# Soft-disc layer of a four-layer kernel: from pairs of blocks to columns of four, sums of exponentials as products with ones, the quotient at the result copy, values through DRAM

## The chip, the cores and the metric
The kernel runs on one core of one Trainium2 chip. The metric is the device time of one execution in microseconds (us). All data are float32.

## What is computed
Four residual layers work one after another on 8 images of 32 x 32 tokens with 256 channels. Each is `x = x + layer(groupnorm(x))`. The change lies in the last one, a windowed attention with a soft disc as mask. Cut to what matters:

```python
def _L3_conv_ref(x, w_qkv, w_qn, w_kn, w_wp, b_wp, w_on, w_out):   # 8 heads of 32 channels, window 7 x 7
    qkv = silu(x @ w_qkv.T)
    q, k, v = split(qkv, 3, axis=-1)
    q = apply_rope(rms_norm(q, w_qn));  k = apply_rope(rms_norm(k, w_kn))
    wp = silu(x @ w_wp.T + b_wp)                      # two numbers per token and head
    width, sharp = sigmoid(wp_1) * max_dist + 0.5, sigmoid(wp_2) * 9.5 + 0.5
    k_win, v_win = unfold2d(k), unfold2d(v)           # zero padding of 3 on each side
    scores = einsum('blhd,blwhd->blhw', q, k_win) * D ** -0.5
    soft_mask = sigmoid((width - rel_dist) * sharp)
    attn = softmax(scores - (1.0 - soft_mask) * 10000.0, axis=-1)
    out = rms_norm(einsum('blhw,blwhd->blhd', attn, v_win), w_on)
    return silu((out + v) @ w_out.T)
```

## The kernel before
**Layers 0 to 2** (`layer0`, `layer1`, `layer2`) are not touched. Layer 2 is a windowed attention too, and it already works in steps of a column of four blocks (`NearStream`, L1655 to L1768): scores L1677, logits L1688, exponentials L1700, quotient on POOL L1705, transposes L1720 with their copies L1724, products with the values L1741, result copy L1748. Its values go through DRAM (stores L1959, fetches of windows L1763).

**Layer 3** is `layer3` (from L2075) with `DiscStream` (from L1771). Channels stand on the partitions and tokens on the free axis. An image's 1024 tokens are 16 blocks of 8 x 8, in 4 columns of 4. The work is cut into 16 chunks J: image b = J // 2 and half of the heads c = J % 2 (4 heads of 32 channels, so 128 partitions). A chunk has 8 groups; a group n is a pair of blocks one above the other, with 128 queries in all on the partitions, so there are 128 groups. Each block sees a window of 14 x 14 = 196 keys.

A group goes through these stages:
- `soft` (L2217, ACT): four tanh, one per head, that write the mask from the distances of a window; width and sharpness of a query are bias and scale.
- `masked` (L2224, POOL): adds the window's hard limits for all four heads at once.
- `scores` (L1802, PE): 8 products, 2 blocks by 4 heads, into four PSUM banks `s`.
- `logits` (L1815, DVE): per head, scores plus mask into the tile `e`, with the minimum as accumulated output `mx`.
- `exps` (L1825, ACT): per head the exponential in place, with the row's sum as accumulated output `su`. The profile shows the reading of that accumulator as an instruction of its own, ACTIVATION_READ_ACCUMULATOR.
- `divide` (L1832 DVE, L1833 POOL): reciprocal of the 4 sums, and e times it.
- `turn` (L1843 PE, L1848 DVE): 4 heads by 2 parts of transposes in two PSUM banks `pt`, each copied to `pts`. A part is 112 keys: 8 rows of 14. The tile e has a row of 14 zeros ahead of the 196 columns and another behind them, so two parts cover the window of either block.
- `values` (L1859 PE, L1867 DVE): 12 products of the turned weights with the values into one bank `o` (4 heads by the three value tiles that the pair's rows touch), and two copies of a block each to the result `oT`.

The values of a chunk are prepared so: `project` makes `vT`; `in_strips` (L2275, POOL, two copies) lays it out in four strips of 14 columns with padding; five units `vturn` (L1876 PE, L1881 DVE) transpose 20 tiles of 112 keys into `v`.

Other work of a chunk: six `project` units (L2141 PE, tanh `half_silu` L2126 on ACT, then DVE L2151 or L2153 from the PSUM bank, squares on POOL L2161); `roots` (sums of squares L2236 and L2243 on PE, and at once a table load, logarithm L2251 and exponential L2252 on ACT); `head_scale` (L2260 PE, L2265 DVE), twice with two banks each. Per image: `load`, group norm (`gn`), `normed` (L418), `discs` (L2174 and after), `tail_sq` (L2289), `tail_scale` (L2295, L2300, L2303), `output` (L2311, L2318, L2320) and `reload`.

**What sets the order.** The block is recorded with `tc.manual_schedule`: PE, ACT, DVE and POOL execute in the order in which the Python code calls them. All PSUM tiles of layer 3 come from one ring of eight banks: an allocation waits until the eighth one before it is released. The loop (L2431) takes group n through a staggered pipeline: scores and logits of n + 3, exponentials of n + 1, quotient of n, turn of n - 2, values of n - 3, mask of n + 5. Between them stand the other units: `Fillers` (L439) holds them with a due time in steps, and `units(at)` emits those that are due. A unit that has a second half (DVE and POOL work that waits for PE or ACT) returns it, and `finish` calls it at the next such point. Transfers are issued by SP in the order of recording, each behind its own waits.

Of the kernel before, what the change touches and what calls it, by code (L numbers as in the profile page):

```python
# [1770 lines left out]
class DiscStream(Stream):  # L1771

# [5 lines left out]
    def __init__(self, K, wk, cp, pp, pairs, n_img, ebufs):  # L1780
        super().__init__(K, wk, pp, pairs, n_img, ebufs)
        self.slots, self.s, self.su = 20, {}, {}
        shape = [P, 4, 2 * self.PART]
        self.tiles = [cp.tile(shape, F32, name=f"e{i}") for i in range(ebufs)]

# [6 lines left out]
    def prob(self, n):  # L1792
        return self.tile(n)[:, :, self.ROW : self.ROW + NWIN]

    def scores(self, n):
        b, c, t = self.groups[n]
        s = [self.ring(f"s{j}") for j in range(4)]
        q, k = self.q[b, c], self.k[b, c]
        for g in range(2):
            for j in range(4):  # L1800
                ch = slice(32 * j, 32 * j + 32)
                self.nc.tensor.matmul(  # L1802
                    grid(s[j][64 * g : 64 * g + 64, :NWIN], self.ROW),
                    q[ch, 64 * t.block(g) : 64 * t.block(g) + 64],
                    k[ch, t.krs[g] : t.krs[g] + self.ROW, t.kc : t.kc + self.ROW],
                    start=True, stop=True,
                )
        self.s[n] = s

    def logits(self, n):  # L1810

        s, e = self.s.pop(n), self.prob(n)
        self.mx[n] = self.wk.tile([P, 4], F32, name="mx", bufs=self.ebufs)
        for j in range(4):
            self.nc.vector.tensor_tensor_reduce(  # L1815
                e[:, j], in0=s[j][:, :NWIN], in1=e[:, j], scale=MASK_SCALE,
                scalar=3.0e38, op0=ALU.add, op1=ALU.min,
                accum_out=self.mx[n][:, j : j + 1],
            )

    def exps(self, n):
        mx, e = self.mx.pop(n), self.prob(n)
        su = self.su[n] = self.wk.tile([P, 4], F32, name="su", bufs=4)
        for j in range(4):
            self.nc.scalar.activation(  # L1825
                e[:, j], e[:, j], AF.Exp, scale=-1.0, bias=mx[:, j : j + 1],
                accum_out=su[:, j : j + 1],
            )

    def divide(self, n):  # L1830
        e, su = self.prob(n), self.su.pop(n)
        self.nc.vector.reciprocal(su, su)  # L1832
        self.nc.gpsimd.tensor_mul(e, e, su.unsqueeze(2).to_broadcast([P, 4, NWIN]))  # L1833

    def turn(self, n, i):

        if i == 0:
            self.pts[n] = self.wk.tile([P, 2, HALF], F32, name="pts", bufs=2)
        ps = self.ring("pt")
        for j in range(2):  # L1840
            for k in range(2):
                at = (2 * j + k) * P
                self.nc.tensor.transpose(  # L1843
                    ps[: self.PART, at : at + P],
                    self.tile(n)[:, 2 * i + j, k * self.PART : (k + 1) * self.PART],
                    self.K.ident,
                )
        self.nc.vector.tensor_copy(self.pts[n][: self.PART, i, :], ps[: self.PART, :])  # L1848

    def values(self, n):  # L1850
        b, c, t = self.groups[n]
        pts = self.pts.pop(n)
        v, at = self.v[b, c], 5 * t.col + t.rows[0]
        o = self.ring("o")

        for k, q0, o0, w in ((1, 64, 0, P), (0, 0, 64, 64), (2, 192, 0, 64)):
            for j in range(4):
                p0 = (j % 2) * 2 * P + q0
                self.nc.tensor.matmul(  # L1859
                    o[32 * j : 32 * j + 32, o0 : o0 + w],  # L1860
                    v[: self.PART, at + k, 32 * j : 32 * j + 32],
                    pts[: self.PART, j // 2, p0 : p0 + w],
                    start=k == 1, stop=k != 1, skip_group_check=True,
                )
        for g in range(2):
            d = self.o[b, c][:, t.token(g) : t.token(g) + 1]
            self.nc.vector.tensor_copy(  # L1867
                bass.AP(d.tensor, d.offset, [d.ap[0], [SIDE, 8], [1, 8]]),
                o[:, 64 - 64 * g : 128 - 64 * g].rearrange("p (i j) -> p i j", j=8),
            )  # L1870

    def value_unit(self, strips, dst, u):
        ps = self.ring("vt")
        for i in range(4):
            col, r = divmod(4 * u + i, 5)
            self.nc.tensor.transpose(  # L1876
                ps[: self.PART, i * P : i * P + P],
                strips[:, col, 8 * r : 8 * r + 8].rearrange("p i j -> p (i j)"),
                self.K.ident,
            )  # L1880
        return lambda: self.nc.vector.tensor_copy(  # L1881
            dst[: self.PART, 4 * u : 4 * u + 4, :],
            ps[: self.PART, :].rearrange("p (s c) -> p s c", c=P),
        )
# [190 lines left out]
def layer3(tc, K, src, dst, n_img, a, first):  # L2075
    nc = tc.nc
    pairs = disc_pairs()
    with tc.tile_pool(name="l3c", bufs=1, reuse_waits="tile") as cp, tc.tile_pool(
        name="l3w", bufs=1, reuse_waits="tile"
    ) as wk, tc.tile_pool(name="l3p", bufs=1, space=PSUM, reuse_waits="tile") as pp:  # L2080
        x, xq, vT, disc, xr, fac, sqs = {}, {}, {}, {}, {}, {}, {}
# [6 lines left out]
        kpad = [cp.tile([P, PADW, PADW], F32, name=f"kp{i}") for i in range(3)]  # L2088
        strips = cp.tile([P, 4, PADW + 2, 14], F32, name="strips")
        for t in (kpad[0], strips):  # L2090
            nc.gpsimd.memset(t, 0.0)
        st = DiscStream(K, wk, cp, pp, pairs, n_img, 9)
        for i in range(3):
            st.clear(i)
        K.ring = st.ring
# [33 lines left out]
        def project(J, s, h):  # L2129
            b, c = divmod(J, 2)  # L2130
            if h == 0:
                if s == 0:
                    st.q[b, c] = wk.tile([P, L], F32, name="qT", bufs=3)
                elif s == 1:
                    st.k[b, c] = kpad[J % 3]
                else:
                    vT[b, c] = wk.tile([P, L], F32, name="vT", bufs=5)
# [74 lines left out]
        def soft(n):  # L2212
            b, c, t = st.groups[n]
            i, e = pairs.index(t), st.prob(n)
# [7 lines left out]
        def masked(n):  # L2222
            e = st.prob(n)
            nc.gpsimd.tensor_add(e, e, win[:, 1].unsqueeze(1).to_broadcast([P, 4, NWIN]))  # L2224

        def roots(J, b):
# [19 lines left out]
            n = P if heads else 64  # L2248
# [6 lines left out]
        def head_scale(J, s):  # L2255

            ps = [st.ring("fac_ps") for _ in range(2)]
            for h in range(2):
                g = slice(32 * (2 * s + h), 32 * (2 * s + h) + 32)
                nc.tensor.matmul(ps[h], spread[g, s], fac[J][g], start=True, stop=True)  # L2260

            def rest():
                for h in range(2):
                    d = dest(J, s, h)
                    nc.vector.tensor_mul(d, d, part(ps[h]))  # L2265

            return rest

        def in_strips(J):
            b, c = divmod(J, 2)  # L2270
            v = grid(vT[b, c], SIDE)
            for out, first, step, n in ((3, 0, 21, 11), (560, 5, 8, 14)):
                i, o = v[:, 0:1, first : first + 1], strips[:, 0:1, 4:5, 0:1]
                ostep = 3 * 560 - 3 if n == 11 else 560
                nc.gpsimd.tensor_copy(  # L2275
                    bass.AP(o.tensor, o.offset + out, [o.ap[0], [ostep, 2], [14, SIDE], [1, n]]),
                    bass.AP(i.tensor, i.offset, [i.ap[0], [step, 2], [SIDE, SIDE], [1, n]]),
                )

        def vturn(J, u):  # L2280
            b, c = divmod(J, 2)
            if u == 0:
                st.v[b, c] = wk.tile([P, st.slots, P], F32, name="v", bufs=2)
            return st.value_unit(strips, st.v[b, c], u)


# [4 lines left out]
        def tail_scale(J, b, h):  # L2291

            g, hs = slice(32 * h, 32 * h + 32), slice(h * HALF, (h + 1) * HALF)
            ps = st.ring("fac_ps")
            nc.tensor.matmul(ps, ones[g], fac[J][g], start=True, stop=True)  # L2295

            def rest():
                for c in range(2):
                    d = st.o[b, c][:, hs]
                    nc.vector.scalar_tensor_tensor(  # L2300
                        d, d, on[:, c : c + 1], ps, ALU.mult, ALU.mult
                    )
                    nc.gpsimd.tensor_add(d, d, vT[b, c][:, hs])  # L2303
# [29 lines left out]
        def plan_chunk(J):  # L2333

            n, (b, c) = 8 * J, divmod(J, 2)
            if J == 0:
                return
            for i in range(4):
                s, h = 1 - i // 2, i % 2
                fill.add(n - 12 + i / 2, lambda s=s, h=h: project(J, s, h))  # L2340
            for s in range(2):
                fill.add(n - 5 - s, lambda s=s: head_scale(J, s))
            fill.add(n - 8.5, lambda: project(J, 2, 0))
            fill.add(n - 8, lambda: project(J, 2, 1))
            fill.add(n - 6, lambda: in_strips(J))

        def plan_image(b):
            n = 16 * b
            if b:
                fill.add(n - 27.5, lambda: load(b))  # L2350
# [169 lines left out]
```

## Time and profile before

| what | us |
|---|---|
| median of 3 runs | 3138.45 (3135.41 to 3157.48) |
| the profiled execution: its time | 3142.47 |
| its span, first to last instruction | 3140.7 |
| layer 2's last scores | 2356.8 |
| layer 3's first and last scores (start) | 2403.6 and 3090.8 |
| layer 3's first and last products with the values (start) | 2434.4 and 3111.6 |

The mean granted TensorE clock is 0.979 of full speed. Instructions of layer 3 by engine, duration from the groups of 2374 to 3141 us, and start to start where the next instruction of the engine follows without idleness:

| instruction | count | mean duration, us | start to start, us |
|---|---|---|---|
| ACT tanh of the mask, L2217 | 512 | 0.541 | 0.442 |
| ACT exponential L1825 to its accumulator read | 512 | 0.447 | 0.349 |
| ACT accumulator read to the next | 512 | 0.190 | 0.093 |
| ACT table load, L2250 | 18 | 1.283 | |
| POOL mask L2224 | 128 | 1.601 | 1.57 |
| POOL quotient L1833 | 128 | 1.498 | 1.456 |
| DVE logits L1815 (each with its accumulator read) | 512 | 0.354 | 0.28 |
| DVE copy of pts, L1848 | 256 | 0.678 | 0.597 |
| DVE copy of a value unit, L1881 | 80 | 0.678 | 0.598 |
| DVE result copy of a block, L1867 | 256 | 0.212 | 0.132 |
| DVE reciprocal of 128 x 4, L1832 | 128 | 0.166 | 0.085 |
| DVE copy of 128 x 2, L205 | 32 (whole kernel) | 0.145 | 0.063 (least 0.045) |
| DVE 128 x 256 from PSUM, L2153 | 128 | 0.415 | 0.332 |

[...] On PE the profile writes a float32 product as two records and a transpose as one, and neighbouring records of one line as one group with the number of records. "Idle before" with an arrow names what ended the idle time. A wait for a PSUM bank appears as a wait for the instruction that released it.

### The profile page before, as it was taken

The page shows a single profiled execution, that of the slowest core. Times are in us where ns is not written, and L with a number is a line of the kernel's source. Part 1 is how long each engine was busy: PE and PEld are TensorE (multiplying, and loading weights), DVE is VectorE, ACT ScalarE, POOL GpSimd, SP SyncE. Part 2 cuts the span into 40 slices and gives each one's busy share as a digit, 9 for nine tenths or more (in the row PEclk, how much of TensorE's full clock was granted, in tenths as well). Part 3 has the DMA queues.
Part 4 walks back from the last instruction along what each step waited for, and adds up shares of the span by engine and source line. Part 5 has one row for each costly group of instructions (what it writes and reads, how often), then busy time and mean ns, then how long its engine had stood idle before and what let it go on. Part 6 is the DMA issues. An engine that isn't in the chain of part 4 may idle for free. (4 is left out here: it accounts for less than half of the span.)

```text
span 3140.7 us, 76133 instructions
## 1 busy us (share of the span) xinstructions
PE 3009.9 (96%) x29928; PEld 1598.3 (51%) x29928; DVE 2216.1 (71%) x5553; ACT 2136.8 (68%) x4833; POOL 1774.8 (57%) x1169
## 2 busy tenths in 40 slices
PE   7999999999999899999999998999998999999997
PEld 3323233233232344577777775666664555555554
DVE  4776776777868467675655664676775888888885
ACT  3667776676677556665555553776776888888885
POOL 4666666656665111154544454343445787888787
PEclk9999999999999999999999998999999999999998
DMA  3000000000001465877887854334341001111001
GB/s 136 14 28 1 28 21 8 28 14 14 28 1 41 152 237 223 282 204 206 207 208 220 213 155 165 111 105 141 115 127 48 15 19 38 42 42 42 28 29 45
DMA packets 191365, 296.85 MB, mean 95 GB/s; under 512 B 13088, under 2 KB 129888, under 8 KB 182688
## 3 DMA queue, kind: packets, MB, share of 16 engines
q1 hardware_dynamic: 184624, 271.61, 28.5%
q10 hardware_dynamic: 6384, 20.37, 1.9%
q8 instruction: 237, 3.88, 0.5%
q14 instruction: 120, 0.98, 0.1%
HBM read 198.35 MB, written 93.59 MB: 93 GB/s over the span
## 5 line engine op out<-in xcount | busy, mean ns | idle before, releaser
L693 DVE TENSOR_TENSOR e<-s,ret 128x1024 f32<-128x1024 f32 x512 | 602.0, 1217 | 174.5 <-PE s L687 172.0
L700 ACT ACTIVATE ea<-e 128x1024 f32<-128x1024 f32 x512 | 535.5, 1055 | 257.5 <-DVE e L693 235.0
L702 POOL TENSOR_TENSOR ea<-ea 128x1024 f32<-128x1024 f32 x128 | 304.4, 2378 | 284.6 <-ACT ea L700 216.6
L687 PE MATMUL s<-qk,qk 32*128 32x512 f32 x2048 | 302.1, 640 | 4.3 <-POOL qk L570 1.7
L1705 POOL TENSOR_TENSOR e<-e,su 128x616 f32<-128x616 f32 (+2 forms) x128 | 156.9, 1231 | 263.3 <-DVE su L1704 237.3
L739 PE MATMUL num<-e,v 128*32 128x512 f32 x2048 | 271.4, 595 | 0.0
L2217 ACT ACTIVATE e<-win,disc 128x196 f32<-128x196 f32 x512 | 239.0, 541 | 0.2
L1848 DVE COPY pts<-pt 112x512 f32<-112x512 f32 x256 | 173.5, 678 | 84.9 <-PE pt L1843 83.2
L1833 POOL TENSOR_TENSOR e<-e,su 128x784 f32<-128x784 f32 x128 | 191.7, 1498 | 73.5 <-DVE su L1832 36.0
L869 PE MATMUL up_ps<-x,wup 128*128 128x512 f32 x512 | 227.4, 598 | 4.0 <-POOL x L237 3.2
L1825 ACT ACTIVATE e<-e,mx 128x196 f32<-128x196 f32 x512 | 226.9, 447 | 0.0
L2224 POOL TENSOR_TENSOR e<-e,win 128x784 f32<-128x784 f32 x128 | 204.9, 1601 | 25.6 <-ACT e L2217 17.8
L1700 ACT ACTIVATE e<-e,mx 128x154 f32<-128x154 f32 (+2 forms) x512 | 211.7, 420 | 4.5 <-DVE mx L1688 4.5
L712 PE MATMUL sm<-ea,ones 128*32 128x512 f32 x1536 | 208.9, 604 | 1.6 <-POOL ea L702 1.6
L1291 POOL TENSOR_TENSOR decayed<-state,rb 128x520 f32<-128x520 f32 x48 | 50.8, 1059 | 275.3 <-DVE state L1321 155.2
L896 DVE SCALAR_TENSOR_TENSOR cv<-xm,par,cv 128x512 f32<-128x512 f32 x192 | 144.7, 754 | 79.0 <-ACT cv L891 74.3
L2141 PE MATMUL qkv_ps<-xq,w 128*128 128x512 f32 x384 | 194.9, 634 | 4.7 <-DVE v L1881 2.5
L687 PEld LDWEIGHTS s<-qk,qk 32*128 32x128 f32 x2048 | 84.7, 182 | 197.3 <-issue 87.7
L1085 ACT ACTIVATE d<-d,cols 128x128 f32<-128x128 f32 x512 | 163.3, 391 | 13.6 <-POOL d L1076 13.0
L1815 DVE CUSTOM_DVE_ANT_0 e<-s,e 128x196 f32<-128x196 f32 x512 | 153.3, 354 | 12.7 <-POOL e L2224 10.8
L1843 PE MATMUL pt<-idg,e 128*112 128x128 f32 x1024 | 156.4, 283 | 4.2 <-POOL e L1833 2.1
L1843 PEld LDWEIGHTS pt<-idg,e 128*112 128x112 f32 x1024 | 117.2, 138 | 78.7 <-issue 49.1
(238 smaller groups left out, 6640.1 us busy)
## 6 DMA issues: line engine op xcount, KB each, us to landing
d<-l1rows SPq DMA_DIRECT2D x64, 512.0 KB
x<-x SPq DMA_DIRECT2D x25, 1024.0 KB
l1xm<-xm SPq DMA_DIRECT2D x16, 1024.0 KB
l1sz<-sz SPq DMA_DIRECT2D x16, 1024.0 KB
xv<-l1xm SPq DMA_DIRECT2D x32, 512.0 KB
l1xa<-xa SPq DMA_DIRECT2D x16, 1024.0 KB
xa<-l1xa SPq DMA_DIRECT2D x16, 1024.0 KB
rb<-l1rows SPq DMA_DIRECT2D x32, 512.0 KB
```

What stands on the lines that cost most here:

```text
L687: nc.tensor.matmul(s[:, j % 2], qk[b, 1, c][g, kb * P : (kb + 1) * P], qk[b, 0, c][g, h * HALF : (h + 1) * HALF], start=True, stop=True,)
L693: nc.vector.tensor_mul(e[n, i], s, m)
L700: nc.scalar.activation(ea[n, i], e[n, i], AF.Abs)
L702: nc.gpsimd.tensor_add(ea[n, i], ea[n, i], ea.pop((n - 1, i)))
L712: nc.tensor.matmul(acc["sm"][g, :], ones, two[j // 2][:, j % 2, :], start=kb == 0 and k == 0, stop=kb == 4 and k == 2,)
L739: nc.tensor.matmul(acc["num"][g, :], v[b][:, kb, vc], e[n, j // 2][:, j % 2, :], start=kb == 0, stop=kb == 7,)
L869: nc.tensor.matmul(ps, wup[:, kc, m * P : (m + 1) * P], seg(s)[:, kc], start=kc == 0, stop=kc == 1,)
L1700: self.nc.scalar.activation(p[:, j], p[:, j], AF.Exp, scale=-1.0, bias=mx[:, i, j : j + 1], accum_out=su[:, j : j + 1],)
L1825: self.nc.scalar.activation(e[:, j], e[:, j], AF.Exp, scale=-1.0, bias=mx[:, j : j + 1], accum_out=su[:, j : j + 1],)
L1843: self.nc.tensor.transpose(ps[: self.PART, at : at + P], self.tile(n)[:, 2 * i + j, k * self.PART : (k + 1) * self.PART], self.K.ident,)
L2217: nc.scalar.activation(e[:, j], win[:, 0], AF.Tanh, scale=disc[b][:, i, 8 + h : 9 + h], bias=disc[b][:, i, h : h + 1],)
L2224: nc.gpsimd.tensor_add(e, e, win[:, 1].unsqueeze(1).to_broadcast([P, 4, NWIN]))
```

## The change
Only `DiscStream` and `layer3` change.

- A step is a column of four blocks (two pairs), so a chunk has 4 groups and the layer 64. The tile e holds two pairs; there are 5 such tiles (before 9 of half the size). `kpad` has 2 buffers (before 3), `qT` 2 (before 3).
- `scores` makes 16 products into the four banks (a pair at column 0, the other at 256). `logits` has 8 instructions. `exps` has no accumulated output. `divide` is gone, and with it `su` as a tile of 4 columns.
- `turn` works head by head: a bank holds the four transposes of one head, written so that the columns stand by part, then row and query. A column has four such banks.
- `values` makes 20 products with the values into `o` and the same 20 with a tile of ones into `su`; then DVE takes the reciprocal of 128 x 256 sums and multiplies o by it on the way to `oT`.
- The values: two units transpose `vT` by tokens (8 tiles of 128) into `vtok`; `keep` stores it in 8 transfers to a padded image in DRAM (two of them in turn, zeroed at the start of the layer by one transfer each); `fetch` brings, per column, five tiles of 112 keys in five transfers, two steps before its column's turn. `in_strips` is gone.
- `roots` is split: `squares_sum` (PE) is a unit, and table load, logarithm and exponential are recorded at the head of every fourth step, behind the scores and ahead of the exponentials. `head_scale` becomes `head_scales`: four banks at once. `tail_scale` does both halves at once. All due times are in steps of a column.

```diff
-    def exps(self, n):
-        mx, e = self.mx.pop(n), self.prob(n)
-        su = self.su[n] = self.wk.tile([P, 4], F32, name="su", bufs=4)
+    def exps(self, n, g):
+        mx, e = self.mx[n], self.prob(n, g)
         for j in range(4):
             self.nc.scalar.activation(
-                e[:, j], e[:, j], AF.Exp, scale=-1.0, bias=mx[:, j : j + 1],
-                accum_out=su[:, j : j + 1],
+                e[:, j], e[:, j], AF.Exp, scale=-1.0, bias=mx[:, g, j : j + 1]
             )
-    def divide(self, n):
-        e, su = self.prob(n), self.su.pop(n)
-        self.nc.vector.reciprocal(su, su)
-        self.nc.gpsimd.tensor_mul(e, e, su.unsqueeze(2).to_broadcast([P, 4, NWIN]))
...
     def values(self, n):
...
+        b, c, col = self.groups[n]
+        pts, v = self.pts.pop(n), self.v.pop(n)
+        o, su = self.ring("o"), self.ring("su")
+        for d in (o, su):
+            for k, m0, o0, w in (
+                (1, 64, 0, P), (3, 320, P, P), (0, 0, 0, 64), (2, 192, 64, P), (4, 448, 192, 64)
+            ):
+                for j in range(4):
+                    self.nc.tensor.matmul(
+                        d[32 * j : 32 * j + 32, o0 : o0 + w],
+                        v[: self.PART, k, 32 * j : 32 * j + 32] if d is o
+                        else self.ones[: self.PART],
+                        pts[: self.PART, j, m0 : m0 + w],
+                        start=k == 1, stop=k in (0, 2, 4), skip_group_check=True,
+                    )
+        r = self.wk.tile([P, 256], F32, name="rsu", bufs=2)
+        self.nc.vector.reciprocal(r, su[:, 0:256])
+        self.nc.vector.tensor_mul(
+            grid(self.o[b, c], SIDE)[:, :, 8 * col : 8 * col + 8],
+            o[:, 0:256].rearrange("p (i j) -> p i j", j=8),
+            r.rearrange("p (i j) -> p i j", j=8),
+        )
...
+    def fetch(self, n, src):
+        col = self.groups[n][2]
+        v = self.v[n] = self.wk.tile([P, 5, P], F32, name="v", bufs=5)
+        for r in range(5):
+            self.nc.sync.dma_start(
+                v[: self.PART, r, :], src[8 * r : 8 * r + 8, 8 * col : 8 * col + self.ROW, :]
+            )
...
+        def keep(J):
+            t, d = tok.pop(J), padded[J % 2]
+            for u in range(8):
+                nc.sync.dma_start(d[4 + 4 * u : 8 + 4 * u, 3 : 3 + SIDE, :], t[:, u, :])
...
+            for m in range(-2, N + 1):
+                if m + 2 < N:
+                    st.scores(m + 2)
+                if m % 4 == 0:
+                    roots(m // 4 + 1)
+                for g in range(2):
+                    if 0 <= m + 1 < N:
+                        st.exps(m + 1, g)
+                if m + 4 < N:
+                    soft(m + 4, 0)
+                units(m)
+                if m + 2 < N:
+                    st.logits(m + 2)
+                for i in range(2):
+                    if 0 <= m < N:
+                        st.turn(m, 2 * i)
+                        st.turn(m, 2 * i + 1)
+                    finish()
+                    if m + 4 < N:
+                        if i == 0:
+                            soft(m + 4, 1)
+                        masked(m + 4, i)
+                    units(m + 0.25 + i / 4)
+                finish()
+                if 0 <= m - 1 < N:
...
+                    st.values(m - 1)
+                units(m + 0.75)
```

## The prediction
> **What bounds the kernel now.** I read three views: busy time by stretch (of the two attention layers), PE in order of time, and the groups of instructions of layer 3. The last scores of layer 2 are over at 2357 us and layer 3 runs to the end at 3140.7, so the change can touch about 760 us of 3140.7.
>
> Busy time of each engine (columns: stretch and length; PE, PEld, DVE, ACT, POOL busy with instruction counts; TensorE clock; DMA share; GB/s). The first line is layer 2, which already works by columns; the other two are layer 3:
>
> ```profile
> 2200.00:2300.00 100.00, 98.80 (x1614) 67.21 (x1596) 71.60 (x344) 70.90 (x274) 42.51 (x36) 1.00 0.39 121
> ...
> 2441.00:2600.00 159.00, 150.22 (x1649) 88.02 (x1651) 132.57 (x484) 133.44 (x400) 122.39 (x91) 0.94 0.07 23
> 2600.00:3000.00 400.00, 387.62 (x4281) 225.77 (x4274) 337.42 (x1234) 340.81 (x995) 334.50 (x244) 0.97 0.11 35
> ```
>
> In layer 3 PE is busy 97% of the middle, DVE, ACT and POOL 84% each. A busy PE need not be full, so the order of time must say it (start, duration, group, count of records; a product is two records, a transpose one):
>
> ```profile
> 2303.37 1.11 PE L1741 MATMUL o<-pts,v 70*32 70x64 f32 x64
> 2304.41 0.85 PE L1677 MATMUL s<-kT,qT 32*64 32x154 f32 x32
> 2305.19 1.98 PE L1933 MATMUL qkv_ps<-x,w 128*128 128x512 f32 x4
> ...
> 2310.94 0.72 PE L1677 MATMUL s<-kT,qT 32*64 32x121 f32 x32
> 2311.59 0.70 PE L1933 MATMUL qkv_ps<-x,w 128*128 128x512 f32 x1
> ```
> ```profile
> 2707.39 0.65 PE L1859 MATMUL o<-pts,v 112*32 112x128 f32 x24
> 2707.96 0.59 PE L1802 MATMUL s<-kp,qT 32*64 32x196 f32 x16
> 2708.49 1.98 PE L2141 MATMUL qkv_ps<-xq,w 128*128 128x512 f32 x4
> ```
> ```profile
> 2456.81 0.65 PE L1876 MATMUL vt<-idg,strips 128*112 128x128 f32 x4 [1.66 <-DVE v L1881]
> 2457.56 0.62 PE L1843 MATMUL pt<-idg,e 128*112 128x128 f32 x4
> 2460.67 3.78 PE L2141 MATMUL qkv_ps<-xq,w 128*128 128x512 f32 x4 [2.49 <-DVE v L1881]
> ```
>
> Group follows group without a gap (second fence): PE's order is what the middle costs, and I price PE work from start to start. The third fence is what disturbs it: a unit waits for a PSUM bank, and after 2.49 us of idleness the same four records take 3.78 us, not 1.98. That is where the clock of 0.94 to 0.97 comes from.
>
> ```profile
> L1833 POOL TENSOR_TENSOR e<-e,su 128x784 f32<-128x784 f32 x128 | 191.7, 1498 | 73.5 <-DVE su L1832 36.0 <-ACT fac L2252 28.6 <-PE pt L1843 6.3
> L1825 ACT ACTIVATION_READ_ACCUMULATOR e<-e,mx 128x1 f32 x512 | 97.2, 190 | 0.0
> L1876 PE MATMUL vt<-idg,strips 128*112 128x128 f32 x320 | 53.6, 294 | 13.9 <-DVE qT L2151 11.5 <-DVE v L1881 1.7
> L1867 DVE COPY oT<-o 128x64 f32<-128x64 f32 x256 | 44.0, 212 | 0.5 <-PE o L1859 0.5
> L1832 DVE RECIPROCAL su<-su 128x4 f32<-128x4 f32 x128 | 21.3, 166 | 0.0
> ```
>
> Here the reader sees what the change deletes (quotient on POOL, accumulator reads on ACT, strips) and that none of it lies on PE, except the vt units.
>
> **The change, part by part** (16 chunks of 4 columns; 64 columns = 128 pairs).
>
> *Off PE.* POOL loses 191.7 us of quotients and 28.0 us of strip copies. ACT loses 512 accumulator reads; an exponential follows the read 0.09 us later in the order of time, so 46 us. Neither engine is the bound: PE idles little on them, so I count nothing for them. The cover is PE's order; were PE not the bound, ACT's 46 us would come out.
>
> *Products with ones.* A pair's values take 2707.96 − 2707.39 = 0.57 (0.58 typically) for 2048 record-columns (8 records of 128, 16 of 64). Layer 2's 64 records of 64, 4096 record-columns, take 1.04: 0.46 per further 2048. A column now has o and su, 8192: 1.04 + 2 x 0.46 = 1.96, against 2 x 0.58 = 1.16. +0.80 x 64 = +51 us. Upper end: four groups at 0.58, +74. I take +51, since layer 2 shows the growth itself.
>
> *Scores of four blocks at once.* Layer 2's 32 records take 0.78 (5600 record-columns) and 0.65 (4400), so 6272 take 0.85, against 2 x 0.53. −0.21 x 64 = −13 us (ends −18, 0).
>
> *Values through DRAM.* A chunk has 2 transposing units, not 5. A unit costs PE 0.44 from start to start: 48 x 0.44 = −21 us. Their waits go with them: 13.9 us before 80 units, so 8 for 48, and the slow clock behind them about half as much: −12 (ends 0, −28). New are 320 fetches and 128 stores on SP's queue. Layer 2's 42 such fetches took 34.59 us there, 0.82 each: 448 x 0.82 = 367 of 760 us on a queue that else issues some 90 transfers here. The queued loads and outputs behind them come later by one burst at most (8 stores, 7 us); a fetch is asked for three columns (30 us) before its values. Nothing on the path, unless that lead is used up.
>
> *Reciprocal and product on DVE.* Out go 128 small reciprocals (0.085 from start to start), 256 copies (0.13), 48 unit copies (0.60): −11 −34 −29. In come 64 reciprocals of 128x256 and 64 products (0.40, as layer 2's result copy L1748 from start to start). The trace has no large reciprocal. Lower bound: 0.33, as other 128x256 operations (L2153) from start to start. The small one takes 0.085 from start to start, a copy of two elements (L205) typically 0.065 and at least 0.045. If all that is over 0.045 is by element, four elements cost 10 ns each and 256 take 2.6 us, the upper bound; over 0.065, 5 ns each and 1.4 us. I take 1.4, against the typical row. DVE then gains 64 x 1.8 − 74 = +41 us over the layer, from 84% to about 90%: no bound, but a queue. Behind the reciprocal stand the next column's logits and its pts copies, and PE wants o's bank again for the first unit after two turns: 0.85 + 1.02 = 1.87 after su. The bank is free at R + 0.33. With R = 1.4 that is 1.73: hidden, with 0.14 to spare. At 2.6 PE waits 1.06 a column, +68.
>
> [...]
>
> *Roots moved.* Logarithm and root now stand at the head of the next step, behind that step's predecessor's last tanh (out). The square sums' bank is held until then, and eight allocations later the first vt unit wants it. Queue on ACT from out's end: tanh 0.5, table load 1.28, logarithm 0.6 = 2.35; PE has only the scores (0.85) ahead. 1.5 us per chunk, +24 over 16. In every second chunk that step has just 5.6 us of PE work, beside 10 us on ACT, and the wait isn't on the path. I take half: +12 (ends 0, +24).
>
> *Start and end.* Eight more soft masks (0.44 each from start to start) stand before the first roots: +3 (ends 0, 7). At the end su, R and the product add 0.96 + 1.4 + 0.33 − 0.35, the last quotient (1.5) goes: +1 (ends −2, 4).
>
> Sum: +51 −13 −21 −12 +12 +3 +1 = **+21 us**. The profiled execution took 3142.47 (span 3140.7), so 3163.5 there. It lies 4.0 above the runs' median 3138.45; the median becomes **3159.5**.
>
> **Rivals.**
> *A, PE packs as in layer 2.* For: fewer bank handovers (10 a column besides the units, before 14), no quotient between exponential and turn, POOL and ACT with slack. Layer 2's stretch shows clock 1.00 and PE idle 1.2%; layer 3's middle 0.97 and 3.1%. Over the 676 us from first to last values that is 20 + 13 us, and the roots' wait (12) goes: 21 − 45 = −24, 3114. Against: DVE at 90%, layer 2's is at 72%.
> *B, the reciprocal.* It decides from R = 1.54 on; each 0.1 us beyond costs 6.4 us. In the middle between that point and the upper bound, 2.1, it adds 36: 3195. For: nothing in the trace excludes it. Against: the small row.
> *C, values arrive late.* If fetches stand behind a waiting output on SP by more than their 30 us, each chunk loses perhaps 5 us: 3240. Against: layer 2 fetches eight a column in 7 us columns with a clock of 1.00.
>
> After an idle stretch PE's rate halves in the third fence. [...]
>
> **How the numbers follow.** A measurement of this kernel can tell about 1% (31 us) from no change; faster means below 3107, slower above 3170. Forecast 0.38 (own range 3135 to 3185: 0.29 within 1%, 0.09 slower); A 0.32 (3095 to 3130: half faster, half within); B 0.22, slower; C 0.04, slower; 0.04 for more gain than any part names, if ACT's 46 us turn out to be on the path. Faster 0.20, same 0.45, slower 0.35. Range 3095 to 3205: A's lower end, and B's price on the forecast; beyond it C and the ends of B added to all others.
>
> **What would show it.** PE groups: o and su together 1.96 us from start to start, scores 0.85, vt idle well under 13.9. The group of the large reciprocal: 1.5 us mean; if it reads above 1.6, B. PE's wait before the first vt unit put down to the logarithm's line, 1.5 us in half of the chunks. Clock in the middle of the layer: 0.97 for the forecast, 1.00 for A. No wait of o's products for the fetched v. The forecast falls if PE is no longer busy over 95% of the middle.

## The result, and the profile after

In the views PE is TensorE, PEld its loads of weights, DVE VectorE, ACT ScalarE, POOL GpSimd; SP issues the transfers. Kernels of the experiments have line numbers of their own.

The changed kernel takes 3189.8 us (median of 4 runs, 3184.76 to 3194.1); the kernel before, on the same chip, 3144.6 (3135.41 to 3157.48). The ratio is 1.0149 (95% interval 1.0105 to 1.0193): slower by 1.5%, inside the range that was given, but 30 us above the number 3159.5, and beyond the forecast's "within 1%". The profiled executions are 3192.3 and 3140.7 us long, 51.6 apart: the first scores start 1.1 later, the 63 columns from the first scores to those of the last column take 727.6 instead of 682.7, and what follows takes 5.6 more. So the change costs where the columns are.

The windows of the changed kernel (columns as in the prediction's first fence): layer 2, early layer 3, and the middle of layer 3.

```profile
2200.00:2300.00 100.00, 98.79 (x1592) 68.15 (x1591) 70.83 (x333) 70.72 (x274) 42.70 (x36) 1.00 0.38 118
2441.00:2600.00 159.00, 146.44 (x2054) 94.60 (x2057) 139.04 (x417) 119.70 (x274) 72.61 (x54) 0.94 0.17 50
2600.00:3000.00 400.00, 374.48 (x4878) 233.18 (x4878) 331.10 (x981) 289.19 (x642) 189.72 (x141) 0.93 0.22 68
```

Layer 2 is the same. In the middle of layer 3 ACT and POOL fell from 340.81 and 334.50 us to 289.19 and 189.72, as the change means to; but PE is busy for 94% (before 97%) at a clock of 0.93 (before 0.97). PE was to gain order and lost it.

The groups of layer 3 in the changed kernel (count | busy, mean ns | idle time before, and what ended it):

```profile
L1869 DVE RECIPROCAL rsu<-su 128x256 f32<-128x256 f32 x64 | 112.1, 1752 | 14.0 <-PE su L1861 14.0
L1870 DVE TENSOR_TENSOR oT<-o,rsu 128x256 f32<-128x256 f32 x64 | 27.2, 425 | 2.2
L2150 PE MATMUL qkv_ps<-xq,w 128*128 128x512 f32 x384 | 212.3, 684 | 17.3 <-DVE rsu L1869 11.9 <-ACT xq L418 3.5 <-DVE pts L1850 1.9
L1845 PE MATMUL pt<-idg,e 128*112 128x128 f32 x1024 | 147.4, 287 | 22.2 <-DVE rsu L1869 6.7 <-DVE oT L2315 5.9 <-ACT fac L2266 5.6
L2276 PE MATMUL fac_ps<-fac,spread 32*128 32x512 f32 x128 | 48.9, 771 | 12.5 <-DVE rsu L1869 7.0 <-ACT fac L2267 4.1 <-DVE mx L1824 1.5
L1880 PE MATMUL vt<-idg,vT 128*128 128x128 f32 x128 | 20.8, 289 | 3.1 <-DVE vT L2162 2.9 <-ACT e L1833 0.3
```

The reciprocal takes 1.752 us; the prediction's own sign for its rival B was "above 1.6". PE now waits for its line in three groups: 11.9 + 6.7 + 7.0 = 25.6 us. The vt units, which waited 13.9 us, wait 3.1.

PE in order of time shows what went as planned (start, duration, group, records):

```profile
2728.17 1.09 PE L1861 MATMUL o<-pts,v 112*32 112x128 f32 x40
2729.07 1.06 PE L1861 MATMUL su<-pts,ones 112*32 112x128 f32 x40
2730.06 2.05 PE L2183 MATMUL wp_ps<-w,xq 128*128 128x128 f32 x16
2732.04 0.93 PE L1809 MATMUL s<-kp,qT 32*64 32x196 f32 x32
2732.90 1.09 PE L1845 MATMUL pt<-idg,e 128*112 128x128 f32 x8
```

From start to start, o takes 0.90 and su 0.99, together 1.89 (predicted 1.96); the scores of four blocks take 0.86 (predicted 0.85). In such a column group follows group. The column before it, 17.5 us earlier, shows where it goes wrong. First PE:

```profile
2711.55 1.06 PE L1861 MATMUL su<-pts,ones 112*32 112x128 f32 x40
2712.54 2.05 PE L2183 MATMUL wp_ps<-w,xq 128*128 128x128 f32 x16
...
2717.33 0.65 PE L1845 MATMUL pt<-idg,e 128*112 128x128 f32 x4
2718.75 0.65 PE L1845 MATMUL pt<-idg,e 128*112 128x128 f32 x4 [0.77 <-DVE rsu L1869]
2719.33 3.09 PE L2276 MATMUL fac_ps<-fac,spread 32*128 32x512 f32 x8
2722.35 3.29 PE L2150 MATMUL qkv_ps<-xq,w 128*128 128x512 f32 x4
```

and DVE at the same time:

```profile
2713.49 0.69 DVE L2333 SCALAR_TENSOR_TENSOR th<-th,out_ps 128x512 f32<-128x512 f32 x1 [3.73 <-ACT th L2135]
2714.10 1.28 DVE L1850 COPY pts<-pt 112x512 f32<-112x512 f32 x2
2715.74 0.69 DVE L2333 SCALAR_TENSOR_TENSOR th<-th,out_ps 128x512 f32<-128x512 f32 x1 [0.36 <-ACT th L2135]
2716.34 0.68 DVE L1881 COPY vtok<-vt 128x512 f32<-128x512 f32 x1
2716.94 1.75 DVE L1869 RECIPROCAL rsu<-su 128x256 f32<-128x256 f32 x1
2718.73 0.42 DVE L1870 TENSOR_TENSOR oT<-o,rsu 128x256 f32<-128x256 f32 x1
```

The sums are complete at 2712.6. DVE stands idle at that time, in front of an instruction that waits for a tanh on ACT (3.73 us); then it has five instructions to make ahead of the reciprocal, and starts it at 2716.94, 4.34 us after the sums. The second transposition wants the sums' bank and waits until the reciprocal has ended (2718.69). PE's list names no wait for the product (L1870): what it waits for is the sums' bank. After that wait of 0.77 us the four qkv records take 3.29 us instead of 1.88 to 1.98. The granted clock says why (stretch and length; PE busy with count; clock; DMA share; GB/s):

```profile
2718.20:2721.61 3.41, 2.86 (x12) 1.00 0.62 195
2721.61:2725.02 3.41, 3.41 (x5) 0.50 0.52 145
```

So in this column a late reciprocal costs PE the wait of 0.77 us, and about twice as much again at half clock behind it (half of the 3.41 us at 0.50, in which PE is busy throughout: 1.7).

### The profile page after: what moved, and what is told of

It is laid out like the page before. It is cut to its first block, busy times and chain, and to the rows that moved or that the text cites. A ratio compares the mean times of both kernels' runs of the same rounds, so it can differ in the third digit from the quotient of the medians.

```text
span 3192.3 us, 79244 instructions
## 1 busy us (share of the span) xinstructions
PE 3027.1 (95%) x31784; PEld 1641.4 (51%) x31784; DVE 2259.9 (71%) x5250; ACT 2091.9 (66%) x4321; POOL 1551.4 (49%) x1003
## 5 line engine op out<-in xcount | busy, mean ns | idle before, releaser
L2150 PE MATMUL qkv_ps<-xq,w 128*128 128x512 f32 x384 | 212.3, 684 | 17.3 <-DVE rsu L1869 11.9
L1850 DVE COPY pts<-pt 112x512 f32<-112x512 f32 x256 | 163.4, 683 | 58.6 <-PE pt L1845 58.3
L1833 ACT ACTIVATE e<-e,mx 128x196 f32<-128x196 f32 x512 | 185.6, 447 | 1.4 <-DVE mx L1824 0.9
L1845 PE MATMUL pt<-idg,e 128*112 128x128 f32 x1024 | 147.4, 287 | 22.2 <-DVE rsu L1869 6.7
L869 PEld LDWEIGHTS up_ps<-x,wup 128*128 128x128 f32 x512 | 95.9, 192 | 118.3 <-issue 107.6
L1076 POOL TENSOR_TENSOR d<-cmask,d 128x1024 f32<-128x1024 f32 x64 | 154.0, 2407 | 0.0
```

Source lines behind the costliest of these rows:

```text
L869: nc.tensor.matmul(ps, wup[:, kc, m * P : (m + 1) * P], seg(s)[:, kc], start=kc == 0, stop=kc == 1,)
L1845: self.nc.tensor.transpose(d[:, g, k], self.tile(n)[:, g, j, k * self.PART : (k + 1) * self.PART], self.K.ident,)
L2150: nc.tensor.matmul(ps, w[:, kc, o : o + P], xq[b][:, kc, h * HALF : (h + 1) * HALF], start=kc == 0, stop=kc == 1,)
```

## The experiments

All times are medians, with the ratio to the kernel before on the same chip. The theories at first: **R**, the reciprocal's length sets the loss; **W** (rival), PE's added products do; **L**, the roots' new place costs; **C** (rival), the step of a column itself costs. When R stood, the question was how: **B**, the reciprocal holds two PSUM banks; **O**, its place makes the next logits late; **D** (rival to both), it counts as work on DVE, wherever it stands. **P** is about one experiment alone, the place of a quotient on POOL.

**A copy in the reciprocal's place.** The output is then o times the sums.

```diff
-        self.nc.vector.reciprocal(r, su[:, 0:256])
+        self.nc.vector.tensor_copy(r, su[:, 0:256])
```


> The large reciprocal becomes a copy of the same 128x256 sums; the output is the values times the sums. Theory R (the reciprocal's 1.75 us hold the banks of o and su and the DVE queue behind it): PE's 25.6 us of waits put down to it go, and as much again in slow clock behind them, so about 3194 - 45 = 3150, and the middle's clock rises from 0.93 to 0.96 or more. Rival W (the 64 x 1 us of products with ones on PE are the loss): the time falls by at most 15, to 3180 or above.

3114.77 us, 0.9916 (0.9888 to 0.9944): from 1.5% above the kernel before to 0.8% below it. R, and with a larger gain than was expected: 2.3%, about 73 us, for a DVE instruction that is 1.33 us shorter in 64 columns (85 us). In total that is nearly all of it, but not because each column pays it: the table at the end of this section has three columns of eight that pay 2.9 to 3.9 us and five that pay 0 to 0.8. W falls, since all products with ones are still there. The middle window, the group, and PE in the column that answers to the one above:

```profile
2600.00:3000.00 400.00, 385.43 (x5469) 247.33 (x5467) 325.33 (x1092) 323.52 (x731) 216.51 (x160) 1.00 0.25 73
```
```profile
L1869 DVE COPY rsu<-su 128x256 f32<-128x256 f32 x64 | 26.9, 420 | 15.4 <-PE su L1861 15.4
```
```profile
2683.58 1.08 PE L1845 MATMUL pt<-idg,e 128*112 128x128 f32 x8
2684.60 2.40 PE L2276 MATMUL fac_ps<-fac,spread 32*128 32x512 f32 x8
2686.93 1.98 PE L2150 MATMUL qkv_ps<-xq,w 128*128 128x512 f32 x4
```

No wait at the transposes, and full speed behind them: the clock of the middle is 1.00. In the traces of the two kernels the granted clock is either 1.00 or 0.50. From the layer's first scores to its last it is at 0.50 for 102 us in the changed kernel and for 24 with the copy (61 in the kernel before). If half clock costs at most half of such a stretch, as in the prediction's third fence (3.78 us against 1.98), at most 39 of the 73 us are clock (an estimate from 102 and 24). DVE is as late as before here (it starts the copy 4.34 us after the sums), but 1.3 us less is enough to be in time.

**The reciprocal made twice.**

```diff
         self.nc.vector.reciprocal(r, su[:, 0:256])
+        self.nc.vector.reciprocal(r, su[:, 0:256])
```


> The same reciprocal is made twice. Theory R: each column's wait grows by the whole second reciprocal (1.7 us), 64 x 1.7 = +109, about 3300. Rival W: DVE has 17% of idle time in the middle that takes most of it up, +30 at most, 3225 or less.

3327.18 us, 1.0584 (1.0555 to 1.0614), beyond the 3300 expected: 137 us above the changed kernel, 2.1 a column for 1.75 us of DVE. PE's waits in layer 3 (us in total, times, longest):

```profile
PE qkv_ps L2151 <- DVE rsu L1870: 49.8, 22, 2.9
PE pt L1845 <- DVE rsu L1870: 36.2, 19, 2.8
PE fac_ps L2277 <- DVE rsu L1870: 23.1, 8, 2.9
PE vt L1881 <- DVE rsu L1870: 10.9, 11, 1.0
```

Together 120 us, where the changed kernel has 25.6.

**The roots back behind their square sums.**

```diff
-                fill.add(4 * J - 4.5, lambda J=J, t=t: squares_sum(J, t))
+                fill.add(4 * J - 4.5, lambda J=J, t=t: (squares_sum(J, t), roots(J))[1])
...
-                if m % 4 == 0:
-                    roots(m // 4 + 1)
```


> Table load, logarithm and exponential of the roots are recorded directly behind the square sums again. Theory L (the first unit of a chunk waits for the square sums' bank, my +12): 12 to 24 us faster, 3170 to 3182, and the waits of pt for the logarithm's line (5.6 us) are gone. Theories R and W: no change beyond 6 us either way, or slower because ACT then waits for the sums.

3166.81 us, 1.0081 (1.0052 to 1.011): 0.7% less, some 22 us, as L expected; the two intervals just touch, and the pairs further down show it again. The waits for the reciprocal stay as they were (11.9, 7.3 and 7.0 us). But the two costs are not separate. In the column that answers to the one shown above, DVE's wait for the tanh is 1.74 us instead of 3.73, because table load, logarithm and exponential no longer stand ahead on ACT; the reciprocal starts 2.36 us after the sums instead of 4.34, and such a column takes 15.55 us instead of 18.04 (means as in the table below). The time at half clock falls from 102 to 68 us.

**The quotient before the turn, columns kept.** Accumulators in `exps`, small reciprocals and the quotient on POOL as in the kernel before, no products with ones, the result copied.

```diff
+                accum_out=su[:, j : j + 1],
...
+    def divide(self, n, g):
+        e, su = self.prob(n, g), self.su.pop((n, g))
+        self.nc.vector.reciprocal(su, su)
+        self.nc.gpsimd.tensor_mul(e, e, su.unsqueeze(2).to_broadcast([P, 4, NWIN]))
...
+                    if 0 <= m + 1 < N:
+                        st.divide(m + 1, i)
```


> Columns and values through DRAM stay; sums come from the exponentials' accumulators and the quotient is made on POOL ahead of the turn, as before the change; no products with ones, no large reciprocal. Theories R and W agree: PE loses 0.99 us a column (63 us), DVE the reciprocal: 3194 - 63 - 45 = about 3085, faster than the kernel before. Rival C (the column step itself, with its coarse handovers of banks, is the loss): 3142 or slower in spite of that.

3212.16 us, 1.0219 (1.0194 to 1.0244): against R's expectation. PE's first wait in it:

```profile
PE pt L1852 <- POOL e L1842: 95.9, 35, 5.4
```

The quotient of a column stood in POOL's queue just ahead of that column's turn, behind masks and residual sums. Whether the place was wrong or the column (C) was tested next.

**The same, one column earlier.** Turn and products a column later, a sixth column buffer; one `vtok` buffer instead of two makes the room, and the squares of the output (`tail_sq`) move with them.

```diff
-                    if 0 <= m < N:
-                        st.turn(m, 2 * i)
-                        st.turn(m, 2 * i + 1)
+                    if 0 <= m - 1 < N:
+                        st.turn(m - 1, 2 * i)
+                        st.turn(m - 1, 2 * i + 1)
```


> As the run with the quotient before the turn, but turns and products a column later, with a sixth buffer of columns, so that GpSimd's quotient has a whole column between it and the turn (one vtok buffer fewer makes the room). Theory P (the 95.9 us that TensorE waited for GpSimd's quotient came from its place): these waits fall below 15 us and the time is 3060 to 3110 us, below the kernel before. Rival C (the step of a column itself costs): 3170 us or more with other waits.

3139.74 us, 0.9992 (0.9976 to 1.0008). That wait has left PE's list and 2.3% went with it: the place. C's 3170 us or more are not reached, and with the last run below C falls. The time is still 30 us above the band expected: POOL is busy for 317 of 400 us in the middle, and PE waits for vT (11.0 us) and for squares on POOL (15.5).

**The power of -1 on POOL, from copies of both banks.**

```diff
-        self.nc.vector.reciprocal(r, su[:, 0:256])
+        self.nc.scalar.copy(r, su[:, 0:256])
+        self.nc.vector.tensor_copy(oc, o[:, 0:256])
+        self.nc.gpsimd.tensor_tensor(r, r, self.minus.to_broadcast([P, 256]), ALU.pow)
...
-        self.nc.vector.tensor_mul(
+        self.nc.gpsimd.tensor_mul(
```


> Both banks are copied out (the sums by ScalarE, the products by VectorE), the reciprocal is made on GpSimd as the power of -1 and the product there too. Theory B (the column's pair of banks is held 2.2 us because the reciprocal reads PSUM for 1.75 us; the products with ones and VectorE's total are of second rank): the banks come free after about 0.5 us, TensorE's waits for the reciprocal (25.6 us) are gone and the time is that of the copy in place of the reciprocal, 3115 us (3100 to 3135), the same as the run with copies out and VectorE's reciprocal. Rival D (VectorE's added 1.33 us in each column makes everything behind it late): this run 3115, but the run with VectorE's reciprocal at 3170 or more. If a power of 256 elements is long on GpSimd (2 elements took 702 ns), GpSimd's masks come late: above 3170 with waits for masked bases.

5503.16 us, 1.7513 (1.7465 to 1.7562). It says nothing on B and D, since POOL became the bound:

```profile
L1874 POOL TENSOR_TENSOR rsu<-rsu,minus 128x256 f32<-128x256 f32 x64 | 2632.4, 41131 | 0.0
```

**Copies out, reciprocal still on DVE at once**, and the same **with the roots back**.

```diff
-        self.nc.vector.reciprocal(r, su[:, 0:256])
+        self.nc.scalar.copy(r, su[:, 0:256])
+        self.nc.vector.tensor_copy(oc, o[:, 0:256])
+        self.nc.vector.reciprocal(r, r)
...
-        self.nc.vector.tensor_mul(
+        self.nc.gpsimd.tensor_mul(
```


> Both banks are copied out (the sums by ScalarE, the products by VectorE); the reciprocal stays on VectorE, of the copy, and the product goes to GpSimd. VectorE's time per column is the same as in the changed kernel. Theory B (banks held): 3115 us (3100 to 3135), TensorE's waits put to the reciprocal's line gone. Rival D (VectorE's load): 3170 us or more, with TensorE's waits put to VectorE's other lines.

> The run with copies out, and the roots directly behind their square sums. Theories B and L (the two costs are separate): 23 us below the run with copies out, 3092 us (3075 to 3115), below the kernel before by over 1%. If the two waits cover one another: the same as the run with copies out, within 8 us.

3210.89 us, 1.0217 (1.0193 to 1.0241), and 3165.38, 1.0069 (1.0042 to 1.0096). B's number failed. The waits of the first of the two show that it was no clean test: DVE's reciprocal waits in DVE's order for ACT's copy, which stands in ACT's order, so the bank is still held and DVE is held as well.

```profile
DVE rsu L1872 <- ACT rsu L1870: 25.5, 21, 3.5
```
```profile
PE fac_ps L2279 <- DVE mx L1824: 16.4, 14, 3.3
PE fac_ps L2279 <- ACT rsu L1870: 12.4, 6, 2.3
PE pt L1845 <- DVE mx L1824: 6.4, 14, 1.2
```

The roots' place was worth 46 us here, twice as much as alone: with the sums' copy on ACT, the roots stand in front of more there. That this is the reason was not tried.

**The reciprocal later, from copies that DVE makes.** DVE copies both banks out at once and makes the reciprocal behind the next logits and two copies of turned weights: 0.4 us more work on DVE per column.

```diff
-        self.nc.vector.reciprocal(r, su[:, 0:256])
+        self.nc.vector.tensor_copy(r, su[:, 0:256])
+        self.nc.vector.tensor_copy(oc, o[:, 0:256])
...
+        def rest():
+            self.nc.vector.reciprocal(r, r)
+            self.nc.gpsimd.tensor_mul(
...
-                    st.values(m - 1)
+                    later.append(st.values(m - 1))
```


> VectorE copies both banks out at once (0.42 us each), and makes the reciprocal later, behind the next column's logits and the first two copies of its turns; GpSimd makes the product. VectorE's work per column grows by 0.4 us against the changed kernel; the banks are free early and no instruction of VectorE waits for another engine because of it. Theory D (in the columns with much other work VectorE runs without a gap, and what a column has of it sets the column's time): no gain, 3190 to 3220 us. Theory O (the reciprocal's place ahead of the logits makes these, and with them the banks of the scores, late): 3110 to 3150.

3163.83 us, 1.0081 (1.0063 to 1.0099): 0.7% less with more work on DVE, so D alone is refuted; the 3110 to 3150 of theory O are missed by 14. PE in the column that answers to the two above:

```profile
2701.61 1.08 PE L1845 MATMUL pt<-idg,e 128*112 128x128 f32 x8
2702.63 2.26 PE L2282 MATMUL fac_ps<-fac,spread 32*128 32x512 f32 x8
2704.82 1.98 PE L2156 MATMUL qkv_ps<-xq,w 128*128 128x512 f32 x4
```

No wait, though the reciprocal is as long as ever. The run changes hold and place at once; it was the bank that the changed kernel's row waited for, so B for this column. In the whole layer PE's list has no wait for the copies that now free the banks.

**Half of the copies of turned weights on ACT**: 1.2 us less on DVE per column.

```diff
-        self.nc.vector.tensor_copy(self.pts[n][: self.PART, j, :], ps[: self.PART, :])
+        copy = self.nc.scalar.copy if j % 2 else self.nc.vector.tensor_copy
+        copy(self.pts[n][: self.PART, j, :], ps[: self.PART, :])
```


> The changed kernel with its reciprocal as it is, and two of a column's four copies of turned probabilities on ScalarE: VectorE has 1.2 us less in a column, ScalarE as much more (ScalarE was busy for 289 of 400 us). Theory D (VectorE's work per column): the time falls as it did with a copy in the reciprocal's place, which took 1.4 us out of the column: 3115 to 3140 us. Theories B and O (how long the reciprocal holds its two banks, or where it stands): nothing of that is changed, 3180 to 3200 us; and slower than that if ScalarE waits in order for the transposes.

3174.0 us, 1.0107 (1.0084 to 1.0131): between the two expectations, and its interval meets the changed kernel's. PE waits 11.7 us for the reciprocal (6.9 + 4.8) instead of 25.6, and newly for the copies on ACT:

```profile
PE s L1809 <- ACT pts L1851: 16.3, 14, 2.8
PE qkv_ps L2151 <- DVE rsu L1870: 6.9, 8, 1.0
PE wp_ps L2184 <- ACT pts L1851: 6.8, 5, 1.4
PE pt L1845 <- ACT pts L1851: 5.7, 7, 2.4
```

So a shorter queue ahead of the reciprocal helps as well; how much it is worth alone stays open, because ACT took a new wait on itself.

**Late reciprocal with the roots back, and early quotient with the roots back** (the edits shown, together).

> The run with the reciprocal behind the logits, and the roots directly behind their square sums. If the two costs are separate: 23 us below that run, some 3140 us (3125 to 3150), the kernel before within 1%. If VectorE's added work (0.4 us a column, and 1.75 us for the reciprocal) is by now what sets the columns: 3155 to 3165, no gain from the roots.

> The run with the quotient before the turn and one column earlier, and the roots directly behind their square sums. TensorE's direct wait for the logarithm is 3.2 us in that run, against 5.6 us in the changed kernel. If the roots cost by this wait and by what stands behind them on ScalarE: 13 us less (3.2 of 5.6 parts of 23), 3127 us (3115 to 3135), just below the kernel before. If the roots cost nothing once the columns have a longer way from exponential to turn: 3135 to 3145 us.

The first: 3142.38 us, 0.9994 (0.9978 to 1.001), 21 below the late reciprocal alone (0.9% or 27 us by the ratios, as they ran on two chips), as expected; the changed kernel's loss is gone. The second: 3116.35 us, 0.9919 (0.9887 to 0.9952), 23 below the early quotient alone, where 13 were expected. It beats both kernels: columns and values through DRAM kept, sums by accumulators and the quotient on POOL kept from the kernel before, and the roots left where they were.

Where the columns' time lies, worked out from the traces: the time from one column's scores to the next ones', mean over columns 16 to 47 by their place among eight (an image), us; in the last row, how long after the sums' end the changed kernel starts the reciprocal that the column begins with.

| column mod 8 | 0 | 1 | 2 | 3 | 4 | 5 | 6 | 7 | mean |
|---|---|---|---|---|---|---|---|---|---|
| changed | 12.58 | 11.13 | 10.94 | 18.04 | 8.08 | 13.36 | 6.54 | 17.49 | 12.27 |
| copy for reciprocal | 9.65 | 10.86 | 10.95 | 14.54 | 8.08 | 12.56 | 6.54 | 13.62 | 10.85 |
| late reciprocal | 9.65 | 10.87 | 10.94 | 14.42 | 8.08 | 13.57 | 6.77 | 17.30 | 11.45 |
| late reciprocal, roots back | 9.65 | 10.87 | 10.94 | 13.19 | 8.08 | 13.57 | 6.66 | 15.80 | 11.09 |
| early quotient, roots back | 9.33 | 12.14 | 10.07 | 12.45 | 7.21 | 13.23 | 5.66 | 15.49 | 10.70 |
| delay of the reciprocal | 2.55 | 0.07 | 0.07 | 4.34 | 0.85 | 0.60 | 0.08 | 1.74 | |

The kernel before has a mean of 11.31. The reciprocal costs 2.9 to 3.9 us in columns 0, 3 and 7, the three in which DVE starts it late, 0 to 0.8 in the other five. The late reciprocal, which frees the banks at once, mends columns 0 and 3 wholly. Column 7 stays at 17.30; DVE is busy for 15.7 of it (11.6 of 13.62 with the copy), which speaks for D in that one column and that run (in the changed kernel it is busy for 12.9 of 17.49). That was not tried by itself and stays open. Nor is it DVE's readiness that mends columns 0 and 3: the copies there start as late as the reciprocal did (2.49 and 4.35 us after the sums), but hold the bank for 0.41 us instead of 1.75. In column 7 they even start 4.31 us after the sums, where the reciprocal started 1.74 after them.

## Why the prediction was right or wrong

- *What bounds the kernel now.* Right: PE's order is the cost of the middle, and slow products after waits are what disturbs it (four qkv records took 3.29 us behind the wait of 0.77, with the copy 1.98). One reading was off: in the third fence the granted clock falls to 0.50 at 2458.91, 0.73 us into the wait of 2.49 and 2.1 us after the wait of 1.66, so it did not take 2.49 us of idleness.
- *Products with ones* (+51) and *scores of four blocks* (-13). Right in size: 1.89 us against 1.96, 0.86 against 0.85. What they are worth in the whole time was not measured by itself.
- *Values through DRAM* (-21 -12). Right as far as the profile shows: two units a chunk, their waits 3.1 us; no wait of PE for a fetched v appears in its list. The gain itself was not measured alone.
- *Reciprocal and product on DVE* (0). **The step that failed.** Its R was 1.4; it measured 1.75, and 1.79 from its start to that of the product that needs it. That is past the 1.54 that the text named, so rival B came about; but by B's own price, 6.4 us for each 0.1 us, R = 1.79 would have cost 16 us, and the copy in its place took 2.3%, about 73 us. What was wrong beside the size is "1.87 after su": it lets the reciprocal begin when the sums are complete, in every column alike. In three of eight columns DVE was 1.7 to 4.3 us late already, and there the hold was past its point by more than a microsecond (at the least 1.74 + 1.75 against 1.87), with waits of up to 1.0 us and half clock behind them. Where DVE came within 0.1 us (columns 1, 2 and 6), the same 1.75 us cost 0 to 0.3: the size alone would have cost little. DVE was costed as "no bound, but a queue", and then the queue was left out of the threshold.
- *Roots moved* (+12 of 0 to +24). The size was right, at the upper end: 22 us alone, 21 and 23 in the last two runs, 46 with the sums' copy on ACT. The direct wait for the logarithm is only 5.6 us, and it appears before a transposition (pt), not before the first vt unit. The path that the text left out goes from the roots over the tanh behind them on ACT to DVE, and makes the reciprocal late (4.34 us instead of 2.36). How the 22 us divide between the two is not shown.
- *Start and end* (+3, +1). The start was +1.1. After the last column's scores 5.6 us more pass (60.0 against 54.4); four columns' reciprocals lie there, and with the copy it is 53.6.
- *The sum.* +21 was forecast, +51.6 came in the profiled execution. 73 + 22 for reciprocal and roots leave -43 for all else, where the steps gave +9 (this takes it that the two add, which was not tried with the copy; as the reciprocal is late in part because of the roots, the -43 is rough). So the gain of rival A, that PE packs better, came about as well: with the copy the clock of the middle is 1.00 and a column takes 10.85 us against 11.31 before. Which of A's reasons made it was not tried. That the time fell inside the range at all was luck in part: the forecast left out a gain of the one rival and a loss of the other.
- *What would show it.* "Clock 0.97" was 0.93, and PE is not "busy over 95% of the middle": by that sign the forecast fell, and the reciprocal's "above 1.6" named the reason.

The 1.75 us lie between the 1.4 taken from the small row and the upper bound of 2.6 from the same row: 6.8 ns for each element of a partition, where the product of the same shape takes 1.7.

## What to carry to other kernels

When an instruction in an in-order queue holds a PSUM bank, price the hold from the time at which its engine gets to it, column by column, and not from the time at which its input is ready: a queue that is on average only 83% busy was 4.3 us late in one column of eight. A quotient was cheapest here where it has few elements (4 sums a row instead of 256 a channel: 0.9992 of the kernel before against 1.0149), if it stands a whole step ahead of its reader (1.0219 where it stood just ahead). If a long instruction has to read PSUM, copy the bank out with the engine that needs it next, and put the long one behind the work that others wait for (1.0081 against 1.0149 here).

## What the hardware showed that was not expected

- A power on GpSimd takes 41.1 us for 128 x 256 elements, 161 ns for each element of a partition; the reciprocal on VectorE takes 6.8.
- Two waits of PE of 0.50 and 0.77 us, 2 us apart, were followed by 3.41 us at a granted clock of 0.50: the head scales and the first qkv unit took 6.15 us from start to start, with the copy (one wait of 0.50, clock 1.00 throughout) 4.15. In the 3.41 us before the fall PE was busy for 2.86. What exactly makes the clock fall is not shown.
